# Second pass of a routed filter and expert kernel: earlier preparation of tiles, another order on the gather queue, results stored from the gathered row's buffer

## The chip, the core and the metric

The kernel runs on one core of a Trainium2 chip. The metric is the device time of one execution in microseconds (us). The kernel before was timed three times, and its median is compared with that of the changed kernel.

## What is computed

Input `x` has 16 x 1024 tokens of 512 numbers. Every token is normalised, then goes two ways: through a filter in the frequency domain with a Golay code correction on top of it (`s`), and through the two best of eight experts (`g`). Cut to what matters:

```python
xn = _layernorm(x)
# attention part: a circular filter whose response depends on D, a number from the data
x1 = ifft(fft(xn) * filt(D)).real
bits = (sigmoid(x1 @ W_el + b_el) > 0.5)              # 24 bits a token
s = x1 + golay_correct(bits) @ W_le + b_le
# expert part
probs = softmax(xn @ router_w.T)                      # 8 experts
topk_vals, topk_idx = top_k(probs, 2)
w = topk_vals / (topk_vals.sum() + 1e-6)
ffn = sum over the two chosen e of (xn @ expert_weights[e] + probs[e]) * w[e]
out = x + s * silu(ffn)
```

## The kernel before, in words

**First pass (`pass_1`, lines 919 to 1016).** It streams `x` in 32 blocks, filters every token, works out bits and routing, and leaves three things in DRAM: the filtered rows `yd`, a record of 28 numbers for each token (`recd`: the eight expert weights, the mean, the scale, the bias, the corrected bits) and, for each of the 28 pairs of experts, a list of the tokens that chose it (`lists`). The lists are then read as one order of tokens, pair after pair. `bounds_b` (line 848) and `place_q` (line 855) compute from the counts where place q of that order stands in `lists`: `place_q` does so for 16 tiles of 128 tokens at a time, on DVE.

**Second pass (lines 1023 to 1247).** It works on 128 tiles of 128 tokens in that order. Neighbouring pairs share an expert, so that a tile needs few experts: there are 283 (tile, expert) items, two for each tile and 27 more. The main loop (line 1212) has one turn `i` for each item; `t = i // 2` is the tile that is about to be prepared, and `f = t - 14` the tile that is finished, because the items lag by up to 14 tiles. All engines' instructions are in the order in which this loop emits them (`manual_schedule`), and each engine takes its own in order. What one tile needs, by engine:

- **POOL** issues five indirect DMAs a tile in even turns: the tile's token numbers (`fetch_tok`, `AHEAD_R` = 8 tiles ahead), its rows of `x` and its records (`fetch_x`, `AHEAD_X` = 5 ahead), the filtered rows of the tile that is soon finished (`fetch_y`), and the store of the last finished tile (`put`).
- **DVE** copies the index column for `fetch_tok` (`at`, line 1058), normalises (`normalize`, `AHEAD_N` = 3 ahead), opens the accumulator row (`open_tile`: weights copied, a memset), adds each product into it (line 1141), triples the bits (`triple`), adds the code's part to the filtered row (`mend`, line 1171), and builds the result in six instructions (`combine`, lines 1176 to 1181). Every 16 tiles it runs `place_q`.
- **PE** transposes the normalised tile (`turn`, four transposes, `AHEAD_T` = 2 ahead), does the item's product (line 1133: eight matmul records), transposes the bits into `pc` (`turn_code`, line 1160) and multiplies the corrected bits with `wle3` (`mend`, line 1170).
- **ACT** copies transposed tiles into a ring (`enter`), copies an item's tile out of the ring (`take`, `TAKES` = 3 items ahead), copies `pc` to `ct` (line 1164) and applies silu (`gate`).

The dynamic choices (which expert, which ring place) are register values that PE, ACT and DVE load from SBUF for four items at a time (`load_regs`, line 1108).

**Buffers that matter.** Products and the code product `pw` share five PSUM buffers (`ps_e`), `pc` has one (`ps_c`), transposed tiles two (`ps_x`). In SBUF: 20 buffers for gathered rows (`xg`), 2 for normalised rows (`xn2`), 3 for results (`o`), 27 for records and token numbers, 4 for item copies (`xw`, one more than `TAKES`), 2 for tripled bits.

**Order inside a turn before.** Even turns: (`place_q` every 16 tiles), `fetch_tok`, `fetch_x`, `fetch_y`, `put`, `normalize`, `turn`; then `take`, `enter`, `product`, `turn_code(f)`. Odd turns: `open_tile`, `take`, `product`, `triple(f + 1)`, `mend(f)`, `gate(f)`, `combine(f)`. So the bits of tile f are tripled in the odd turn before, transposed at the end of the even turn, and `mend(f)` needs them, through ACT's `ct`, one product later.

Of the kernel before, what the change touches and what calls it, by code (L numbers as in the profile page):

```python
# [8 lines left out]
F32 = mybir.dt.float32  # L9
BF16 = mybir.dt.bfloat16  # L10
U32 = mybir.dt.uint32
I32 = mybir.dt.int32
# [5 lines left out]
P = 128  # L18
PSUM = bass.MemoryType.PSUM
DRAM = bass.MemoryType.DRAM  # L20
NPAIR = 28
RING = 16
META = 28
# [27 lines left out]
def kernel(  # L51
# [29 lines left out]
    nc = tc.nc  # L81

    E = x.shape[-1]
    H = E // 2
# [8 lines left out]
    NT = N // P  # L93
# [3 lines left out]
    Q = E // 4  # L97
# [5 lines left out]
    bt = ctx.enter_context(tc.tile_pool(name="bt", bufs=1))  # L103
# [19 lines left out]
    mid = p1.enter_context(tc.tile_pool(name="mid", bufs=1))  # L123
# [17 lines left out]
    dbase_r = row_sb[:, NPAIR : 2 * NPAIR]  # L141
# [688 lines left out]


    G = 16
    addrs = [bt.tile([P, G], I32, name=f"addr{t}") for t in range(NT // G)]
    qf = bt.tile([P, NT], F32, name="qf")
    off = bt.tile([P, 3 * NPAIR], F32, name="off")
    step = bt.tile([P, NPAIR], F32, name="step")
    woff = bt.tile([1, NIP], I32, name="woff")
    slot = bt.tile([1, NIP], I32, name="slot")
# [1 line left out]
    md = Group()  # L840
# [7 lines left out]
    def bounds_b():  # L848

        po = ps_g.tile([P, 512], F32, name="pg")[:, 0 : 3 * NPAIR]  # L850
        nc.tensor.matmul(po, md.cnt, ord_sb, start=True, stop=True)
        nc.vector.tensor_copy(off, po)
        nc.vector.tensor_sub(step, dbase_r, off[:, 2 * NPAIR :])

    def place_q(t: int):

        cmp = bt.tile([P, G, NPAIR], F32, name="cmp")
        nc.vector.tensor_tensor(
            cmp,
            qf[:, t : t + G].unsqueeze(2).to_broadcast([P, G, NPAIR]),  # L860
            off[:, 0:NPAIR].unsqueeze(1).to_broadcast([P, G, NPAIR]),
            ALU.is_ge,
        )
        nc.vector.tensor_mul(cmp, cmp, step.unsqueeze(1).to_broadcast([P, G, NPAIR]))
        jump = bt.tile([P, G], F32, name="jump")
        nc.vector.tensor_reduce(jump, cmp, AX.X, ALU.add)
        nc.vector.tensor_add(addrs[t // G], jump, qf[:, t : t + G])

    def takes_a():

        begin, end = off[:, 0:NPAIR], off[:, NPAIR : 2 * NPAIR]
        lo = mid.tile([P, NPAIR], F32, name="lo")
        nc.vector.tensor_scalar(lo, begin, tf[:, 0:1], None, ALU.max)
        hi = mid.tile([P, NPAIR], F32, name="hi")
        nc.vector.tensor_scalar(hi, end, tf[:, 1:2], None, ALU.min)
        nc.vector.tensor_tensor(lo, lo, hi, ALU.is_lt)
        use = mid.tile([P, NE, NPAIR], F32, name="use")
        nc.vector.tensor_mul(use, mem_r, lo.unsqueeze(1).to_broadcast([P, NE, NPAIR]))
        md.takes = mid.tile([P, NE], F32, name="takes")
        nc.vector.tensor_reduce(md.takes, use, AX.X, ALU.max)  # L880
        takes_b = mid.tile([P, NE], BF16, name="takes_b")
        nc.vector.tensor_copy(takes_b, md.takes)

        md.pn = ps_g.tile([P, 512], F32, name="pg")[:, 0:NE]
        nc.tensor.matmul(md.pn, tri_b, takes_b, start=True, stop=True)
# [33 lines left out]
    def pass_1():  # L919
# [84 lines left out]
        bounds_a()  # L1004
        syndrome()
        bounds_b()
        place_q(0)
        correct()
        push(99)
        put_records(NT - GT, GT)  # L1010
# [10 lines left out]


    mp = ctx.enter_context(tc.tile_pool(name="mp", bufs=27))
    xnp = ctx.enter_context(tc.tile_pool(name="xnp", bufs=2))
    xgp = ctx.enter_context(tc.tile_pool(name="xgp", bufs=20))
    w2 = ctx.enter_context(tc.tile_pool(name="w2", bufs=2))
    rings = ctx.enter_context(tc.tile_pool(name="rings", bufs=1))
    ps_x = ctx.enter_context(tc.tile_pool(name="ps_x", bufs=2, space=PSUM))
# [2 lines left out]
    xring = rings.tile([P, RING, KC * P], F32, name="xring")  # L1031
    aring = rings.tile([P, RING, E], F32, name="aring")
    wring = rings.tile([P, RING * 16], F32, name="wring")
    nc.vector.memset(wring, 0.0)

    class Tile:
# [4 lines left out]
    def gather(dst, src, idx, limit):  # L1041
        nc.gpsimd.indirect_dma_start(  # L1042
            out=dst,
            out_offset=None,
            in_=src,
            in_offset=bass.IndirectOffsetOnAxis(ap=idx, axis=0),
            bounds_check=limit - 1,
            oob_is_err=False,
        )
# [12 lines left out]
    def fetch_x(t: int):  # L1062
        k = tiles[t]
        k.x = xgp.tile([P, E], F32, name="xg")
        gather(k.x, xf, k.tok, N)
        k.rec = mp.tile([P, META], F32, name="rec")
        gather(k.rec, recd, k.tok, N)

    def fetch_y(t: int):
# [4 lines left out]
    def normalize(t: int):  # L1074
        k = tiles[t]
        k.xn = xnp.tile([P, E], F32, name="xn2")
        nc.vector.tensor_scalar(  # L1077
            k.xn, k.x, k.rec[:, 10:11], k.rec[:, 11:12], ALU.subtract, ALU.mult
        )
# [9 lines left out]
    def enter(t: int):  # L1089

        nc.scalar.copy(xring[:, t % RING, :], tiles[t].pt)

    def open_tile(t: int):
        k = tiles[t]
        s = t % RING
        nc.vector.tensor_copy(wring[:, s * 16 : s * 16 + NE], k.rec[:, 0:NE])
        nc.vector.memset(aring[:, s, :], 0.0)
# [52 lines left out]
    def triple(t: int):  # L1150

        k = tiles[t]
        k.b3 = w2.tile([P, 3, 32], BF16, name="b3")
        bits = k.rec.bitcast(BF16)[:, BITS : BITS + 32]
        nc.vector.tensor_copy(k.b3, bits.unsqueeze(1).to_broadcast([P, 3, 32]))

    def turn_code(t: int):
        k = tiles[t]
        pc = ps_c.tile([96, P], F32, name="pc")
        nc.tensor.matmul(  # L1160
            pc, k.b3.rearrange("p k l -> p (k l)"), ident_b, start=True, stop=True
        )
        k.ct = w2.tile([96, P], BF16, name="ct")
        nc.scalar.copy(k.ct, pc)  # L1164
# [7 lines left out]

    def combine(t: int):
        k = tiles[t]
        k.o = w2.tile([P, E], F32, name="o", bufs=3)
        nc.vector.tensor_add(k.o[:, 0:Q], k.y[:, 0:Q], k.y[:, Q:H])
        nc.vector.tensor_sub(k.o[:, Q:H], k.y[:, 0:Q], k.y[:, Q:H])
        nc.vector.tensor_sub(k.o[:, H:E], k.o[:, 0:H], k.y[:, H:E])
        nc.vector.tensor_add(k.o[:, 0:H], k.o[:, 0:H], k.y[:, H:E])  # L1179
        nc.vector.tensor_mul(k.o, k.o, aring[:, t % RING, :])  # L1180
        nc.vector.tensor_add(k.o, k.o, k.x)  # L1181

    def put(t: int):
        k = tiles.pop(t)
        dma = nc.gpsimd.indirect_dma_start(  # L1185
            out=of,
            out_offset=bass.IndirectOffsetOnAxis(ap=k.tok, axis=0),
            in_=k.o,
            in_offset=None,
            bounds_check=N - 1,  # L1190
            oob_is_err=False,
        )
        tc.declare_no_dep(dma.ins, group="rows", reason="rows of their own")
        tc.add_to_no_dep_group("rows", dma.ins)

    LAST = NPAIR // 2
    AHEAD_R, AHEAD_X, AHEAD_N, AHEAD_T, TAKES = 8, 5, 3, 2, 3
    with tc.manual_schedule():
        for t in range(AHEAD_R):
            fetch_tok(t)  # L1200
            if 2 <= t and t - 2 < AHEAD_X:
                fetch_x(t - 2)
        load_regs(0)
        for t in range(AHEAD_N):
            normalize(t)
            if t < AHEAD_T:
                turn(t)
                enter(t)
        open_tile(0)
        for i in range(TAKES):  # L1210
            take(i)
        for i in range(NI + 2 * LAST):
            t = i // 2
            f = t - LAST
            if i % (2 * G) == 0 and t + G < NT:
                place_q(t + G)
            if i % 4 == 0 and i + 4 < NIP:
                load_regs(i + 4)
            if i % 2 == 0:
                if t + AHEAD_R < NT:  # L1220
                    fetch_tok(t + AHEAD_R)
                if t + AHEAD_X < NT:
                    fetch_x(t + AHEAD_X)
                if 0 <= f + 2 < NT:
                    fetch_y(f + 2)
                if 0 <= f - 1 < NT:
                    put(f - 1)
                if t + AHEAD_N < NT:
                    normalize(t + AHEAD_N)
                if t + AHEAD_T < NT:  # L1230
                    turn(t + AHEAD_T)
            elif t + 1 < NT:
                open_tile(t + 1)
            if i + TAKES < NI:
                take(i + TAKES)
            if i % 2 == 0 and t + AHEAD_T < NT:
                enter(t + AHEAD_T)
            if i < NI:
                product(i)
            if i % 2 == 0 and 0 <= f < NT:  # L1240
                turn_code(f)
            if i % 2 == 1 and 0 <= f + 1 < NT:
                triple(f + 1)
            if i % 2 == 1 and 0 <= f < NT:
                mend(f)
                gate(f)
                combine(f)
# [86 lines left out]
```

## Time and profile before

| what | value |
|---|---|
| three timed runs, us | 1593.53, 1586.84, 1565.13; median 1586.84 |
| the profiled execution's own time, us | 1558.99 |
| span of its trace, us | 1557.2 |
| mean granted TensorE clock | 0.964 |
| DVE / ACT / POOL busy, share of the span | 75% / 41% / 58% |
| product matmuls L1133 | 2264 records, 1021.3 us busy |
| one indirect DMA on POOL | about 1.0 us |
| DMA engines' mean busy share in the second pass | about 0.33 |

The page of the profile gives, for one execution, each engine's busy time, the span in 40 slices, and groups of instructions with their mean duration in ns. Other answers of the trace list the instructions in order of time: start, duration, engine, line, operation, "out<-in", how many, and in brackets how long the engine had been idle and what ended that ("issue": nothing that the profile shows; "remote": a signal whose sender the profile could not name). The ends of PE's matmuls are modelled, their starts are measured. The first pass fills about 400 us of the span; the first product of the second pass starts at 410.1 us.

### The profile page before, as it was taken

How to read it: one execution, taken by the hardware profiler on the slowest of the kernel's cores; microseconds unless marked ns; L12 is line 12 of the kernel's file. 1: busy time of each engine (PE TensorE's matmuls, PEld its weight loads, DVE VectorE, ACT ScalarE, POOL GpSimd, SP SyncE). 2: the span in 40 equal slices, each digit the busy share in tenths (PEclk: the TensorE clock that was granted, in tenths of full speed). 3: DMA queues.
4: the chain of work that ended last, by engine and by line, in shares of the span. 5: the costliest groups of instructions: out<-in, count | busy, mean ns of one | idle time of the engine just before them, and what ended most of it. 6: DMA issues, size and time to landing. Idle time of an engine off the chain costs nothing.

```text
span 1557.2 us, 20298 instructions
## 1 busy us (share of the span) xinstructions
PE 1408.6 (90%) x4955; PEld 751.6 (48%) x4955; DVE 1168.0 (75%) x3057; ACT 636.2 (41%) x1346; POOL 898.1 (58%) x907
## 2 busy tenths in 40 slices
PE   3998988885699989989898997999999989999997
PEld 2877777663344444434344443444444444444443
DVE  7799999997433668778676866877688778887666
ACT  4988888662122323323232322332333233333221
POOL 1357776675644556656655665666576656664332
PEclk8999999997699999999999999999999999999999
DMA  5997667531111223323323332333233333332211
GB/s 219 330 317 242 216 209 218 169 115 58 46 44 43 77 90 104 106 94 91 103 83 95 105 104 70 101 105 104 83 105 98 101 90 104 106 115 83 81 68 61
DMA packets 91391, 185.04 MB, mean 119 GB/s; under 512 B 21998, under 2 KB 57710, under 8 KB 87182
## 3 DMA queue, kind: packets, MB, share of 16 engines
q0 software_dynamic: 43472, 104.51, 22.3%
q1 hardware_dynamic: 46702, 78.07, 15.2%
q10 hardware_dynamic: 1104, 1.17, 0.2%
q8 instruction: 44, 0.72, 0.2%
q14 instruction: 69, 0.57, 0.1%
HBM read 112.86 MB, written 70.84 MB: 118 GB/s over the span
## 4 chain that ended last, share of the span: by engine, by line
PE 58%; DVE 21%; issue 12%; ACT 3%; POOL 3%; another core or an unknown queue 2%; DVEq 1%; DMA 0%; ACTq 0%; POOLq 0%
PE pe L1133 47%; PE pt L1085 3%; PE py L548 2%; DVE sd L518 2%; DVE pp L466 2%; PE pe L1170 1%; POOL yg L1042 1%; POOL out L1185 1%; DVE sd L521 1%; DVE ex L573 1%; ACT no L483 1%; PE pt L530 1%; DVE o L1180 1%; PE py L545 1%
## 5 line engine op out<-in xcount | busy, mean ns | idle before, releaser
L1133 PE MATMUL pe<-w_sb,xw 128*128 x2264 | 1021.3, 601 | 0.0
L1133 PEld LDWEIGHTS pe<-w_sb,xw 128*128 128x128 f32 x2264 | 415.8, 193 | 463.6 <-issue 463.1
L1141 DVE SCALAR_TENSOR_TENSOR aring<-pe,wring,aring 128x512 f32 x283 | 211.8, 749 | 262.8 <-PE pe L1133 133.6
L1042 POOL DMA_INDIRECT tok<-lists,at x120 | 130.8, 1090 | 245.0 <-DVE at L1058 232.2
L1148 ACT ACTIVATE aring<-aring,rec 128x512 f32<-128x512 f32 x128 | 92.5, 723 | 439.0 <-DVE aring L1141 359.8
L1122 ACT COPY xw<-xring 128x512 f32 x283 | 172.5, 611 | 78.5 <-PE pe L1133 58.6
L1042 POOL DMA_INDIRECT yg<-yd,tok x128 | 135.7, 1060 | 107.8 <-DVE o L1179 67.8
L795 POOL DMA_INDIRECT lists<-tok,dst x128 | 130.3, 1018 | 61.4 <-DVE mo L808 37.7
L1185 POOL DMA_INDIRECT out<-o,tok x128 | 132.5, 1035 | 54.0 <-issue 37.5
L1042 POOL DMA_INDIRECT xg<-in_x,tok x128 | 129.0, 1008 | 46.4 <-issue 39.6
L523 POOL TENSOR_TENSOR mm<-xt 128x256 f32<-128x256 f32 x128 | 99.8, 780 | 94.7 <-PE pt L530 58.3
L1042 POOL DMA_INDIRECT rec<-recd,tok x128 | 129.2, 1009 | 40.0 <-issue 39.7
L548 PE MATMUL py<-cm,pmt 128*128 128x288 f32 x512 | 149.1, 415 | 0.0
L1164 ACT CAST ct<-pc 96x128 bf16<-96x128 f32 x128 | 33.4, 261 | 268.7 <-PE pc L1160 157.9
L551 ACT ACTIVATE yb<-py,rec 128x640 f32<-128x640 f32 x128 | 101.5, 793 | 29.6 <-PE py L548 15.7
L548 PEld LDWEIGHTS py<-cm,pmt 128*128 128x128 f32 x512 | 92.5, 194 | 14.0
L1180 DVE TENSOR_TENSOR o<-o,aring 128x512 f32<-128x512 f32 x128 | 88.6, 692 | 14.0 <-issue 0.5
L1085 PEld LDWEIGHTS pt<-ident,xn 128*128 128x128 f32 x512 | 66.5, 147 | 66.8 <-issue 44.2
L1085 PE MATMUL pt<-ident,xn 128*128 128x128 f32 x512 | 82.4, 286 | 12.8 <-DVE xn L1077 9.3
L1181 DVE TENSOR_TENSOR o<-o,xg 128x512 f32<-128x512 f32 x128 | 88.8, 694 | 4.4
L483 ACT ACTIVATE no<-xt,sum 128x512 bf16<-128x512 f32 x128 | 91.0, 711 | 0.3 <-DVE pp L466 0.2
L1171 DVE TENSOR_TENSOR yg<-pe,yg 128x512 f32<-128x512 f32 x128 | 87.2, 681 | 0.0
(226 smaller groups left out, 1597.4 us busy)
## 6 DMA issues: line engine op xcount, KB each, us to landing
xt<-in_x SPq DMA_DIRECT2D x32, 1024.0 KB
yd<-yb SPq DMA_DIRECT2D x32, 1024.0 KB
w_sb<-in_expert_w SPq DMA_DIRECT2D x8, 1024.0 KB
lists<-tok,dst POOLq DMA_INDIRECT x128
xg<-in_x,tok POOLq DMA_INDIRECT x128
rec<-recd,tok POOLq DMA_INDIRECT x128
yg<-yd,tok POOLq DMA_INDIRECT x128
out<-o,tok POOLq DMA_INDIRECT x128
```

What stands on the lines that cost most here:

```text
L483: nc.scalar.activation(no, xts[g // TPT][:, g % TPT, :], AF.Square, bias=k.sum[:, j : j + 1], scale=-float(E), accum_out=k.sq2[:, j : j + 1],)
L523: nc.gpsimd.tensor_tensor(m, xr[:, 0:H], xr[:, H:E], ALU.subtract)
L548: nc.tensor.matmul(py[:, 1, 0 : X + H], pmt[:, 2 + c, :], cm[:, c, :], start=(c == 0), stop=(c == 1))
L551: nc.scalar.activation(y_room(g), py[:, :, 0:WY], AF.Copy, scale=k.rec[:, j, 11:12])
L795: dma = nc.gpsimd.indirect_dma_start(out=lists, out_offset=bass.IndirectOffsetOnAxis(ap=st.dst[:, j : j + 1], axis=0), in_=tok[:, t0 + j : ...
L1042: nc.gpsimd.indirect_dma_start(out=dst, out_offset=None, in_=src, in_offset=bass.IndirectOffsetOnAxis(ap=idx, axis=0), bounds_check=limit - 1,
L1085: nc.tensor.transpose(k.pt[:, c * P : (c + 1) * P], k.xn[:, c * P : (c + 1) * P], ident)
L1122: nc.scalar.copy(xw.rearrange("p c t -> p (c t)").unsqueeze(1), xring[:, bass.ds(regs.pop(("a", i)), 1), :],)
L1133: nc.tensor.matmul(pe.unsqueeze(1), xw[:, c, :], w_sb[:, bass.ds(e, 1), c, :], start=(c == 0), stop=(c == KC - 1),)
L1141: nc.vector.scalar_tensor_tensor(acc, pe.unsqueeze(1), wring[:, bass.ds(regs.pop(("c", i)), 1)], acc, ALU.mult, ALU.add,)
L1180: nc.vector.tensor_mul(k.o, k.o, aring[:, t % RING, :])
L1185: dma = nc.gpsimd.indirect_dma_start(out=of, out_offset=bass.IndirectOffsetOnAxis(ap=k.tok, axis=0), in_=k.o, in_offset=None, bounds_check ...
```

## The change

It moves preparation earlier and reorders the loop. Rows are normalised 4 tiles ahead instead of 3 and gathered 6 ahead instead of 5; items are copied 4 ahead instead of 3; bits are tripled three tiles before they are finished instead of one, and transposed one tile earlier (`CODE = 1`). The store `put(f - 1)` is emitted first in the even turn instead of after `fetch_y`, and `enter` comes before `take`. The result is built in one scratch row `mix`, and its last addition writes into `k.x`, the gathered row's own buffer, from which `put` stores; the three buffers `o` are gone. `place_q` uses `mix` (or a first-pass buffer) as its scratch and makes its addresses in two rotating buffers; `bounds_b` copies its sums in two instructions instead of one. Buffers: `xn2` 3, `xg` 22, `rec` 22, `xw` 5, `b3` 3.

```diff
-    addrs = [bt.tile([P, G], I32, name=f"addr{t}") for t in range(NT // G)]
+    addrs = {}
-    off = bt.tile([P, 3 * NPAIR], F32, name="off")
+    begin = bt.tile([P, NPAIR], F32, name="begin")
@@ bounds_b
-        nc.vector.tensor_copy(off, po)
-        nc.vector.tensor_sub(step, dbase_r, off[:, 2 * NPAIR :])
-
-    def place_q(t: int):
-        cmp = bt.tile([P, G, NPAIR], F32, name="cmp")
+        nc.vector.tensor_copy(begin, po[:, 0:NPAIR])
+        md.off = mid.tile([P, 2 * NPAIR], F32, name="off")
+        nc.vector.tensor_copy(md.off, po[:, NPAIR:])
+        nc.vector.tensor_sub(step, dbase_r, md.off[:, NPAIR:])
+
+    def place_q(t: int, room):
+        cmp = room[:, 0 : G * NPAIR].rearrange("p (g k) -> p g k", k=NPAIR)
+        jump = room[:, G * NPAIR : G * (NPAIR + 1)]
...
-        jump = bt.tile([P, G], F32, name="jump")
         nc.vector.tensor_reduce(jump, cmp, AX.X, ALU.add)
+        addrs[t // G] = bt.tile([P, G], I32, name="addr", bufs=2)
@@ buffers of the second pass
-    xnp = ctx.enter_context(tc.tile_pool(name="xnp", bufs=2))
-    xgp = ctx.enter_context(tc.tile_pool(name="xgp", bufs=20))
+    xnp = ctx.enter_context(tc.tile_pool(name="xnp", bufs=3))
+    xgp = ctx.enter_context(tc.tile_pool(name="xgp", bufs=22))
+    mix = rings.tile([P, E], F32, name="mix")
-        k.rec = mp.tile([P, META], F32, name="rec")
+        k.rec = mp.tile([P, META], F32, name="rec", bufs=22)
-        k.b3 = w2.tile([P, 3, 32], BF16, name="b3")
+        k.b3 = w2.tile([P, 3, 32], BF16, name="b3", bufs=3)
@@ combine, put
-        k.o = w2.tile([P, E], F32, name="o", bufs=3)
-        nc.vector.tensor_add(k.o[:, 0:Q], k.y[:, 0:Q], k.y[:, Q:H])
...
-        nc.vector.tensor_mul(k.o, k.o, aring[:, t % RING, :])
-        nc.vector.tensor_add(k.o, k.o, k.x)
+        nc.vector.tensor_add(mix[:, 0:Q], k.y[:, 0:Q], k.y[:, Q:H])
...
+        nc.vector.tensor_mul(mix, mix, aring[:, t % RING, :])
+        nc.vector.tensor_add(k.x, mix, k.x)
-            in_=k.o,
+            in_=k.x,
@@ the loop
-    AHEAD_R, AHEAD_X, AHEAD_N, AHEAD_T, TAKES = 8, 5, 3, 2, 3
+    AHEAD_R, AHEAD_X, AHEAD_N, AHEAD_T, TAKES = 8, 6, 4, 2, 4
+    CODE = 1
             if i % (2 * G) == 0 and t + G < NT:
-                place_q(t + G)
+                place_q(t + G, mix)
             if i % 2 == 0:
+                if 0 <= f - 1 < NT:
+                    put(f - 1)
                 if t + AHEAD_R < NT:
                     fetch_tok(t + AHEAD_R)
                 if t + AHEAD_X < NT:
                     fetch_x(t + AHEAD_X)
                 if 0 <= f + 2 < NT:
                     fetch_y(f + 2)
-                if 0 <= f - 1 < NT:
-                    put(f - 1)
...
+            if i % 2 == 0 and t + AHEAD_T < NT:
+                enter(t + AHEAD_T)
             if i + TAKES < NI:
                 take(i + TAKES)
-            if i % 2 == 0 and t + AHEAD_T < NT:
-                enter(t + AHEAD_T)
             if i < NI:
                 product(i)
-            if i % 2 == 0 and 0 <= f < NT:
-                turn_code(f)
-            if i % 2 == 1 and 0 <= f + 1 < NT:
-                triple(f + 1)
+            if i % 2 == 0 and 0 <= f + CODE < NT:
+                turn_code(f + CODE)
+            if i % 2 == 1 and 0 <= f + CODE + 2 < NT:
+                triple(f + CODE + 2)
```

More of the change, by code (lines that the diff above doesn't have):

```diff
@@ L860, in place_q @@
             qf[:, t : t + G].unsqueeze(2).to_broadcast([P, G, NPAIR]),
-            off[:, 0:NPAIR].unsqueeze(1).to_broadcast([P, G, NPAIR]),
+            begin.unsqueeze(1).to_broadcast([P, G, NPAIR]),
             ALU.is_ge,
@@ L864, in place_q @@
         nc.vector.tensor_mul(cmp, cmp, step.unsqueeze(1).to_broadcast([P, G, NPAIR]))
-        jump = bt.tile([P, G], F32, name="jump")
         nc.vector.tensor_reduce(jump, cmp, AX.X, ALU.add)
+        addrs[t // G] = bt.tile([P, G], I32, name="addr", bufs=2)
         nc.vector.tensor_add(addrs[t // G], jump, qf[:, t : t + G])
     def takes_a():
-        begin, end = off[:, 0:NPAIR], off[:, NPAIR : 2 * NPAIR]
+        end = md.off[:, 0:NPAIR]
         lo = mid.tile([P, NPAIR], F32, name="lo")
@@ L1006, in pass_1 @@
         bounds_b()
-        place_q(0)
+        place_q(0, mid.tile([P, E], F32, name="cmp"))
         correct()
@@ L1174, in combine @@
         k = tiles[t]
-        k.o = w2.tile([P, E], F32, name="o", bufs=3)
-        nc.vector.tensor_add(k.o[:, 0:Q], k.y[:, 0:Q], k.y[:, Q:H])
-        nc.vector.tensor_sub(k.o[:, Q:H], k.y[:, 0:Q], k.y[:, Q:H])
-        nc.vector.tensor_sub(k.o[:, H:E], k.o[:, 0:H], k.y[:, H:E])
-        nc.vector.tensor_add(k.o[:, 0:H], k.o[:, 0:H], k.y[:, H:E])
-        nc.vector.tensor_mul(k.o, k.o, aring[:, t % RING, :])
-        nc.vector.tensor_add(k.o, k.o, k.x)
+        nc.vector.tensor_add(mix[:, 0:Q], k.y[:, 0:Q], k.y[:, Q:H])
+        nc.vector.tensor_sub(mix[:, Q:H], k.y[:, 0:Q], k.y[:, Q:H])
+        nc.vector.tensor_sub(mix[:, H:E], mix[:, 0:H], k.y[:, H:E])
+        nc.vector.tensor_add(mix[:, 0:H], mix[:, 0:H], k.y[:, H:E])
+        nc.vector.tensor_mul(mix, mix, aring[:, t % RING, :])
+        nc.vector.tensor_add(k.x, mix, k.x)
     def put(t: int):
```

## The prediction

> **What bounds the kernel now.** I read the page first, then the busy time by stage, PE's waits, the chain of waits and the instructions in order of time. Busy time by stage (PE, PEld, DVE, ACT, POOL, then clock, DMA share, GB/s):
>
> ```profile
> 410.00:541.00 131.00, 130.85 (x356) 60.96 (x355) 58.97 (x133) 34.98 (x59) 62.67 (x62) 0.98 0.19 51
> 541.00:1400.00 859.00, 811.81 (x2287) 377.60 (x2286) 646.63 (x1476) 269.69 (x521) 537.18 (x521) 0.98 0.33 98
> 1400.00:1547.00 147.00, 147.00 (x381) 65.55 (x379) 104.36 (x218) 41.01 (x81) 50.12 (x43) 1.00 0.23 76
> ```
>
> The second pass is bound by PE, which is without a gap before 541 us and after 1400 and loses 47 us between: just the stretch in which POOL issues all five DMAs a tile. An undisturbed tile takes 7.64 us of PE there, as two pieces of the chain of waits show (start, duration):
>
> ```profile
> 894.22 3.49 PE pe L1133 x8
> ...
> 901.86 3.49 PE pe L1133 x8
> ```
>
> The same view gives 7.31 us for the first 14 tiles, which finish none, and the order of time gives 7.20 at the end, without transposes. 14 x 7.31 + 112 x 7.64 + 15.5 x 7.20 = 1069.6 us; from the first product at 410.1 that ends at 1479.7. The last product really ends at 1547.1: **67 us lost**. After it 10.1 us of tail follow, so the floor of the span is 1490. PE's waits in this pass:
>
> ```profile
> PE pe L1170 <- issue: 27.3, 7, 4.8
> PE pe L1170 <- DVE aring L1141: 11.2, 2, 5.6
> PE pt L1085 <- DVE xn L1077: 4.2, 8, 3.0
> PE pc L1160 <- DVE b L1155: 2.3, 2, 1.7
> PE pe L1170 <- ACT ct L1164: 1.9, 1, 1.9
> ```
>
> Ten stops at the code product L1170 make 40.4 us, eight transposes and two bit transposes 6.5. The remaining 20 us are matmuls at half clock after stops. What ends a stop shows in the order of time:
>
> ```profile
> 666.00 1.13 POOL L1042 DMA_INDIRECT tok<-lists,at  x1 [4.13 <-DVE at L1058]
> ...
> 672.68 1.03 POOL L1042 DMA_INDIRECT tok<-lists,at  x1 [0.30 <-DVE xn L1077]
> ...
> 677.91 0.22 PE L1160 MATMUL pc<-ident_b,b 128*96 128x128 bf16 x1
> 677.97 3.65 PE L1133 MATMUL pe<-w_sb,xw 128*128 x8
> ...
> 684.58 1.01 POOL L1185 DMA_INDIRECT out<-o,tok  x1 [0.30 <-issue]
> 686.19 0.75 DVE L1141 SCALAR_TENSOR_TENSOR aring<-pe,wring,aring 128x512 f32 x1 [6.74 <-remote]
> 686.89 0.26 ACT L1164 CAST ct<-pc 96x128 bf16<-96x128 f32 x1 [10.08 <-remote]
> ...
> 687.21 0.61 PE L1170 MATMUL pe<-wle,ct 96*128 96x512 bf16 x1 [5.59 <-DVE aring L1141]
> ```
>
> PE finished the product and `pc` at 678.1, yet DVE and ACT, both idle, act on it only at 686.2 and 686.9. So PE's signal is held for 8 us, PE does the next product, and then waits for `ct`, not for DVE as the bracket says: two of five `ps_e` buffers are taken. Each of the ten stops has such a hold beside it. What they share is POOL: a tile's five DMAs start 1.31 us apart (6.54 us); in quiet tiles POOL then waits 0.77 or 1.8 us for DVE's `at`. Here `place_q` made it wait 4.13, it fell behind, and 15 DMAs ran without a pause (19.6 us) until 685.6. The signals came 0.6 us later. Six long runs follow `place_q`, the others an odd pause of POOL or an earlier hold. That a long run causes the hold is my inference; the trace has no row for it.
>
> **What the Trainium skill says.** (1) *Perfetto Trace Analysis*, "Tensor Engine Instruction (MATMUL, LD_WEIGHTS)": the end of a matmul is estimated, and its signal goes out only once PSUM has acknowledged the write. That permits a late signal; an 8 us one no page explains. (2) *TensorE: Matmul & The Clock Gate*, "What's actually happening": the clock halves after an idle window of about 3.4 us and recovers after a busy one. The trace agrees: after the stop above, the four transposes take 1.06 us against 0.60. (3) *GPSIMD Engine Reference*, "4. When to use GPSIMD": POOL's cores themselves write the descriptors of its DMAs; here 1.0 us of POOL for each. (4) *DMA: Bandwidth & Descriptors*, "Anatomy of one DMA — SWDGE (gpsimd) path": 2.0 us plus bytes / 436e3. My estimate for a 256 KB store is 2.6 us; no view here gives the landing.
>
> **The change part by part.**
>
> *Bits a tile earlier.* `mend(f)` no longer needs the `pc` of the same tile. After a hold begins at `pc`, PE does as before one product, then also `mend` (0.22), transposes (0.44) and the next product (3.44), before the next `pc` needs the single `ps_c` buffer, which ACT has not emptied. That is 4.1 us more cover. The ten stops are 4.83, 5.59, 1.86, 4.84, 4.83, 5.58, 2.71, 2.50, 2.74 and 4.84; less 4.1 each, at least nothing, 5.9 us stay. **Saved: 34.5.** The cover needs `xw` four ahead (ACT is held too) and `xn` made a tile before: both are in the change. PSUM allows five products or code products. If the cover were gone, the 34.5 would be back.
>
> *Normalised rows a tile earlier.* The 6.5 us of PE's waits on `xn` and bits come when `place_q` (0.62 x 3 + 0.17 = 2.0 us) delays DVE by about 3 us; the new lead is 7.6. **Saved: 6.5.**
>
> *Half clock.* With stops under 1.5 us PE should not cool: of the 20 us I take **17**; bounds 0 and 20.
>
> *Result in `mix`, store from `xg`.* The same six DVE instructions, no DMA removed. New wait: `fetch_x(t + 6)` needs the buffer whose store was issued in the tile before, seven DMAs (9.2 us) earlier; it lands after an estimated 2.6. Cost 0, hidden by those DMAs; if landing took over 9 us, POOL's rows, records and `yg` behind it would be late too. `mix` has only DVE as its user, in order: 0.
>
> *`put` first.* It waits for DVE's last addition L1181, and `fetch_tok` (then `xg`, `rec`, `yg`) is queued behind; but `at` follows L1181 on DVE anyway, so nothing is later. After `place_q` the store fills part of the pause: I work out store, pause of 1.9, four DMAs, pause of 1.4, then ten without a pause (12.9 us) and one of 0.8, instead of fifteen. SP has no part in this pass; ACT's queue only swaps `enter` and `take`, and `take` now waits for the transposes, which precede the product: 0. `yg` goes 1.3 us later in a tile and is needed two tiles on: 0.
>
> *One more small copy at the end of the first pass.* The nearest row, COPY of 128x8, has 197 ns: +0.2. Two more DMAs in the prologue (2.6 us) lie beside the first five products (17 us).
>
> *What is late next.* After a hold PE no longer paused, so DVE is up to 7.5 us behind (the product's 3.44 and the 4.1). A DVE-bound tile takes 6.5 us (L1181 starts at 671.46 and 677.92), so DVE regains 1.1 a tile; meanwhile POOL (6.54) runs without pause, and a new hold may follow. The trace shows such followers: the holds of 746, 1084 and 1215, where PE stopped least, each had another 26 to 28 us later. Bounds: 0, and the second rival. I charge **20 us**, about a third of the way.
>
> Sum: 1557.2 - 34.5 - 6.5 - 17 + 20 + 0.2 = 1519 span; with the 1.8 us around it 1521 against 1558.99. The timed median lies 28 us above that execution. I take this surplus for more holds and carry over a small part, 4 us, because each costs less: **1525**.
>
> **Rivals.**
> - *Nothing follows.* Without the 20 us: 1505. For it: most holds follow `place_q`, whose run is broken up. I count it with the forecast: together 0.55, between 1495 and 1545.
> - *Holds follow each other.* POOL runs 12 us until the hold, DVE lives 7.5 on older signals, the begun tile ends: four tiles (26.1) and a pause of 6.5 until DVE's next L1181. 8.15 us a tile: 112 x 0.51 = 57 over the floor, 1490 + 57 + 2 = 1549. For it: the followers above. Against it: `rec` or `xg` pauses break runs. 0.22, 1545 to 1575.
> - *No effect.* Leads are useless because DVE, held as well, fills `ps_e`: about 1587. Against it: three free buffers at the stop. 0.08.
> - *Slower.* POOL becomes the bound: DVE stands from the beginning of each hold, three tiles (19.6) and a pause of 6.5, 8.70 us a tile: 112 x 1.06 = 119, 1611, plus cold clock up to 1650. It decides above 8.49 us a tile, where 1586.84 is reached. Against it: a DVE that is behind has old signals to work on. 0.15.
>
> **Numbers.** The likeliest is 1525, its own range 1495 to 1545; all cases give 1495 to 1600, with about 1.5 in 10 outside. A measurement of this kernel tells about 2% from no change: under 1555 is faster, 0.55 + 0.4 x 0.22 = 0.64; over 1618 slower, 0.6 x 0.15 = 0.09; the same 0.27.
>
> **What would show it.** Right: stops at L1170 below 10 us in all, PE over 97% between 541 and 1400, no wait on `xn` or bits, few half-clock slices, holds still there ("remote" before L1141), the run after `place_q` ten DMAs. Wrong: new long waits of PE at L1160, L1133 or L1170, POOL without pauses, tiles of 8.1 us or more, or POOL waiting before `xg` for a store.

## The result, and the profile after

The changed kernel took 1555.37 us (median of 20 runs, 1532.4 to 1568.6), the kernel before beside it 1585.01: 1.9% less, where I forecast 1525 and 3.9%. Over the undisturbed executions alone the ratio is 0.986 (95% interval 0.982 to 0.990), a gain of 1.4%; the profiled execution (1557.48 us, span 1555.7) counts as disturbed by that rule, but it lies 2 us from the median and is read as typical. The engines are called by their names in the profile: PE is TensorE, DVE VectorE, ACT ScalarE, POOL GpSimd.

Busy time by stage of the changed kernel (columns as in the prediction):

```profile
410.00:541.00 131.00, 131.00 (x359) 61.18 (x358) 61.39 (x139) 36.12 (x63) 66.16 (x65) 0.99 0.21 54
541.00:1400.00 859.00, 818.93 (x2287) 379.44 (x2286) 646.10 (x1471) 262.18 (x517) 537.25 (x519) 0.97 0.33 97
1400.00:1547.00 147.00, 145.81 (x376) 64.86 (x375) 106.59 (x222) 42.04 (x84) 44.26 (x44) 1.00 0.24 76
```

The middle stretch holds the same 2287 records of PE as before: the two profiled executions (1558.99 and 1557.48 us) are nearly equal, and the 30 us between the medians are not in these traces. I expected PE above 97% there; it has 95.3%. The waits in that stretch before (us in total, times, longest):

```profile
POOL tok L1042 <- DVE at L1058: 177.8, 81, 9.1
...
ACT ct L1164 <- remote: 87.3, 11, 10.1
...
DVE aring L1141 <- remote: 65.5, 14, 6.7
```

And after:

```profile
DVE aring L1145 <- remote: 109.9, 23, 8.3
ACT ct L1168 <- remote: 102.0, 16, 10.9
POOL out L1188 <- DVE xg L1184: 89.3, 16, 8.3
...
POOL out L1188 <- DVE at L1062: 72.2, 19, 8.4
...
PE pc L1164 <- ACT ct L1168: 31.7, 8, 6.1
```

The stops at the code product are gone, and stand one instruction earlier, at the bit transpose L1164, whose single PSUM place ACT has not emptied. The waits for held signals ("remote") have grown: 110 us before DVE's L1145 and 102 before `ct`, against 65.5 and 87.3. And POOL, which used to wait a little in most tiles, now waits rarely and long. In order of time:

```profile
575.35 1.12 POOL L1188 DMA_INDIRECT out<-xg,tok  x1 [5.28 <-DVE at L1062]
...
582.04 1.18 POOL L1188 DMA_INDIRECT out<-xg,tok  x1 [0.30 <-issue]
...
588.79 1.02 POOL L1188 DMA_INDIRECT out<-xg,tok  x1 [0.30 <-issue]
...
595.37 1.07 POOL L1188 DMA_INDIRECT out<-xg,tok  x1 [0.30 <-issue]
...
603.82 0.75 DVE L1145 SCALAR_TENSOR_TENSOR aring<-pe,wring,aring 128x512 f32 x1 [8.27 <-remote]
603.85 0.26 ACT L1168 CAST ct<-pc 96x128 bf16<-96x128 f32 x1 [4.42 <-remote]
604.17 0.26 PE L1164 MATMUL pc<-ident_b,b 128*96 128x128 bf16 x1 [3.27 <-ACT ct L1168]
...
610.12 1.13 POOL L1188 DMA_INDIRECT out<-xg,tok  x1 [8.41 <-DVE at L1062]
```

Four tiles of POOL without a pause (20 DMAs until 601.7), a hold, a stop of PE, DVE late, POOL waits 8.41 us for it, and the next run begins. Between 541 and 1340 us, 25 runs of eleven to twenty DMAs (gaps under 0.45 us) hold 423 of POOL's DMAs; before, 13 runs of ten to fifteen held 172. This is the prediction's rival "holds follow each other".

### The profile page after: what moved, and what is told of

It reads as the page before. It is cut to its first block, busy times and chain, and to the rows that moved or that the text cites. A ratio compares the mean times of both kernels' runs of the same rounds, so it can differ in the third digit from the quotient of the medians.

```text
span 1555.7 us, 20156 instructions
## 1 busy us (share of the span) xinstructions
PE 1415.1 (91%) x4955; PEld 754.2 (48%) x4955; DVE 1169.9 (75%) x3058; ACT 630.9 (41%) x1346; POOL 896.4 (58%) x907
## 4 chain that ended last, share of the span: by engine, by line
PE 48%; DVE 22%; issue 15%; another core or an unknown queue 5%; POOL 4%; ACT 4%; DVEq 1%; DMA 0%; POOLq 0%; ACTq 0%
PE pe L1137 38%; PE py L548 2%; PE pt L1089 2%; POOL yg L1046 2%; DVE sd L518 2%; DVE pp L466 2%; DVE aring L1145 2%; DVE sd L521 1%; ACT no L483 1%; DVE ex L573 1%; DVE mix L1183 1%; PE pt L530 1%; PE pe L1174 1%; PE py L545 1%
## 5 line engine op out<-in xcount | busy, mean ns | idle before, releaser
L1137 PE MATMUL pe<-w_sb,xw 128*128 x2264 | 1034.3, 607 | 1.2 <-DVE aring L1145 1.2
L1145 DVE SCALAR_TENSOR_TENSOR aring<-pe,wring,aring 128x512 f32 x283 | 211.8, 749 | 258.4 <-remote 111.2
L1188 POOL DMA_INDIRECT out<-xg,tok x128 | 137.4, 1073 | 290.9 <-DVE xg L1184 182.1
L1046 POOL DMA_INDIRECT tok<-lists,at x120 | 124.8, 1040 | 85.6 <-DVE at L1062 53.1
L1095 ACT COPY xring<-pt 128x512 f32<-128x512 f32 x128 | 73.1, 571 | 102.8 <-PE pt L1089 44.2
L1183 DVE TENSOR_TENSOR mix<-mix,aring 128x512 f32<-128x512 f32 x128 | 88.6, 692 | 14.7 <-DVE mix L1182 0.9
L1184 DVE TENSOR_TENSOR xg<-mix,xg 128x512 f32<-128x512 f32 x128 | 88.8, 694 | 4.4
L1175 DVE TENSOR_TENSOR yg<-pe,yg 128x512 f32<-128x512 f32 x128 | 87.3, 682 | 4.0 <-remote 2.4
```

What stands on the lines that cost most here:

```text
L1046: nc.gpsimd.indirect_dma_start(out=dst, out_offset=None, in_=src, in_offset=bass.IndirectOffsetOnAxis(ap=idx, axis=0), bounds_check=limit - 1,
L1137: nc.tensor.matmul(pe.unsqueeze(1), xw[:, c, :], w_sb[:, bass.ds(e, 1), c, :], start=(c == 0), stop=(c == KC - 1),)
L1145: nc.vector.scalar_tensor_tensor(acc, pe.unsqueeze(1), wring[:, bass.ds(regs.pop(("c", i)), 1)], acc, ALU.mult, ALU.add,)
L1183: nc.vector.tensor_mul(mix, mix, aring[:, t % RING, :])
L1188: dma = nc.gpsimd.indirect_dma_start(out=of, out_offset=bass.IndirectOffsetOnAxis(ap=k.tok, axis=0), in_=k.x, in_offset=None, bounds_check ...
```

## The experiments

**Theory H:** where POOL issues DMAs for longer than some 12 us without a pause, signals of PE are held; the change left PE no stop in which DVE catches up, so runs follow on runs. **Rivals:** C, the single PSUM place of the bit transpose is what costs; P, POOL's own work is the bound; L, the longer leads remove waits that have nothing to do with holds.

The experiments ran on different chips, and this proved to be the largest effect of all. I name the chips by the time of the *unchanged* kernel before, taken beside each experiment:

| chip | kernel before, us | experiments |
|---|---|---|
| A | 1579.6 | e1 to e4 |
| B | 1495.9, 1495.8 | e5 to e8, e13 to e15 |
| C | 1495.1, 1494.9 | e9 to e12, e17 |
| D | 1585.3 | e16 |
| E | 1565.6 | e18 |

B and C were met twice and gave the same time both times; A, D and E were met once each. Ratios below are to the kernel before on the same chip, with 95% intervals. The changed kernel itself was timed in two places only: for the result above, and on chip C. Where times on A, D and E are set against its 1555, that is across comparisons.

### On chip A: pause, fewer DMAs, second place, store first

**e1**, the changed kernel with a pause of POOL:

```diff
                 if t + AHEAD_R < NT:
+                    for _ in range(4):
+                        nc.gpsimd.memset(rest, 0)     # 128x16 scratch
                     fetch_tok(t + AHEAD_R)
```

> The changed kernel with four memsets of a 128x16 scratch by GpSimd ahead of each tile's fetch of its row numbers, so that GpSimd's DMAs never run on for more than one tile (five DMAs, 6.5 us) without 0.8 us or so between two of them. Theory H (GpSimd's uninterrupted run of DMAs, when longer than some 12 us, holds back the signals of TensorE; the change removed TensorE's stop and so let runs follow on runs): the waits of ScalarE and VectorE for a remote signal, 102 and 110 us, fall below 30 us, the stops of TensorE at the bit transpose (41 us) below 12, and the time falls from 1555 to 1490 to 1515. Rival C (the stops come from the single PSUM place of the bit transpose, whatever GpSimd does): the waits stay and the time is 1550 to 1570. Rival P (GpSimd's own work is the bound): 0.4 us more a tile makes it slower, about 1555 + 112 x 0.4 = 1600.

Measured: 1508.8 us, ratio 0.954 (0.947 to 0.961). No wait for a remote signal is left between 541 and 1400 us, PE is busy for 856 of 859 us at full clock, and POOL's DMAs come in fives with 1.31 us between:

```profile
541.00:1400.00 859.00, 856.17 (x2448) 399.09 (x2447) 697.29 (x1573) 282.47 (x557) 617.69 (x988) 1.00 0.35 103
```

With work added to POOL the kernel is 47 us below the change alone (ratio 0.954 here, 0.986 for the change beside its own kernel before). So P falls, and C falls as the cause of the holds: the waits went although the single place stayed.

**e2** leaves out the gather of the records from the 17th tile on and uses those of the first 16 again (`if t < 16: gather(k.rec, ...) else: k.rec = recs[t % 16]`), so that POOL issues four DMAs a tile:

> The changed kernel with the gather of the records left out from the 17th tile on (records of the first 16 tiles are used again, so the output's weights and corrections are those of other rows). GpSimd issues four DMAs a tile, 5.2 us, in place of five, 6.5. Theory H: GpSimd has over 1.5 us a tile to wait, so no run is long, the holds go, and the time is 1485 to 1515. Rival C: as the changed kernel, 1545 to 1565. Rival P (GpSimd's work is the bound): also faster, near 1490, so this run tells H and P from C only; the pause run tells H from P.

Measured: 1494.4, ratio 0.946 (0.939 to 0.953); no remote wait, PE busy for 859.00 of 859 us. As H expects.

**e3**, `ps_e` 5 to 4 buffers, `ps_c` 1 to 2:

> The changed kernel with two PSUM places for the bit transpose and four, in place of five, for the products. Rival C: the stops at the bit transpose (41 us) go and the time falls to about 1515 to 1525. Theory H: a hold of about 8 us still stops TensorE at the next place it needs (four products' places now last 2.2 us less), so the sum of TensorE's waits stays at 40 to 60 us and the time within 1545 to 1570.

Measured: 1542.4, ratio 0.979 (0.970 to 0.987). The stops at L1164 are gone, but PE now stops at the products, 22.8 us for ACT's `xw` and 9.1 for DVE's accumulation. The waits for remote signals stay (99.8 us before DVE's L1145, 60.3 before `ct`). The place decides where PE stops, not whether a hold comes. H's numbers were a little high: PE's waits come to 32 us where I expected 40 to 60, and the time, 13 us under the 1555 of the changed kernel, is slightly below H's range and well above C's.

**e4**, the kernel before with only `put` moved to the front:

> The kernel before with one edit of the change alone: the store of a finished row is issued first among a tile's DMAs instead of last. My prediction put the gain of the change on the longer leads and counted the order of the store as small: 1575 to 1590 expected. A rival: the store's wait for VectorE now stands ahead of all fetches, breaks GpSimd's runs differently and takes a good part of the change's 30 us: 1555 to 1570. A third: without the longer leads it makes more pauses and fewer holds but delays fetches: 1590 to 1610.

Measured: 1529.1, ratio 0.970 (0.962 to 0.978): better than the whole change and below all three expectations. Held signals are much shorter here:

```profile
DVE aring L1141 <- remote: 41.6, 13, 5.0
...
ACT ct L1164 <- remote: 20.6, 6, 6.5
```

Six of its long runs are of ten DMAs (about 13.2 us), among them those after `place_q` at 665.84, 794.58 and 1174.41, as the prediction had worked out for the store's move. But eleven others have 14 to 20 DMAs, and its 17 runs of ten or more hold 236 DMAs between 541 and 1340 us, more than the 172 of the kernel before. A run of twenty (723.3 to 750.6) held one signal of DVE for 4.1 us and stopped PE not at all. So H in the form of run lengths does not explain why e4 is fast; that stays open.

### Chips without holds

**e5**, the change with `put` back behind `fetch_y` (leads and `mix` without the store's move); **e6**, before + pause; **e7**, before + store first + pause; **e8**, the change with `CODE = 0`:

> The changed kernel with the store put back to the end of a tile's DMAs, as in the kernel before: the longer leads and the scratch row without the move of the store. The store's move alone gave 1529, less than the whole change (1555). Theory H: the leads take TensorE's stop away, and that stop was what let VectorE catch up and GpSimd pause; with the store last as well there are the fewest pauses, so the holds follow each other: 1570 to 1600, no gain over the kernel before. Rival L (the leads are worth 26 us or more by themselves, as my prediction worked out, and the two edits only overlap): 1525 to 1560.

> The kernel before with the four memsets of GpSimd ahead of each tile's row numbers, and nothing else. Theory H: without long runs of GpSimd's DMAs there are no holds and nothing for the longer leads to cover; the time is that of the changed kernel with the pause, 1500 to 1520. Rival L (the short leads stop TensorE by themselves): ten stops at the code product and the waits for normalised rows stay, 1540 to 1570.

> The kernel before with the store first and with the pause: next to the changed kernel with the pause (1509) it differs by the longer leads and the scratch row only. Theory H: 1500 to 1520, the leads are worth under 10 us when nothing is held. Rival L: 1525 to 1545.

> The changed kernel with the bit transpose back in the tile of its code product, all other leads as changed. If the earlier bit transpose is the lead that lets runs follow on runs (TensorE again stops at the code product in a hold), the time comes near that of the store's move alone: 1520 to 1540. If another lead does it (rows gathered and normalised a tile earlier), it stays at 1545 to 1570.

All four met chip B, where the kernel before took 1495.9. Measured: e5 1493.6 (0.998), e6 1517.2 (1.014), e7 1511.8 (1.011), e8 1493.5 (0.998). So where nothing is held, the leads are worth 2 us, and the pause *costs* 16 to 21. The expectations for e5 and e8 were meant for a chip with holds and aren't tested by this; e6 and e7 came within H's numbers and below L's, but where nothing is held that says nothing about holds.

**e9**, the changed kernel as it is; **e10**, **e11** and **e12** repeat e5, e8 and e6:

> The changed kernel as it is, beside the kernel before on the chip of this call. The chips of the two calls so far differ: on the first the kernel before took 1580 and signals of TensorE were held, on the second it took 1496 and GpSimd's runs of up to 15 DMAs (20 us) held nothing. Theory H': the hold is this chip's answer to GpSimd's long runs, and the change's gain is only what it saves of the holds. Where the kernel before takes 1496, expected 1488 to 1497 (under half a per cent); where it takes 1580, 1550 to 1560. Rival L (the leads remove waits that have nothing to do with holds): 15 us or more also where the kernel before takes 1496.

> The changed kernel with the store back at the end of a tile's DMAs, again, for the chip where signals are held. Theory H there: the leads alone give 1560 to 1600, since TensorE's stop no longer lets VectorE catch up and GpSimd pause. Rival L there: 1525 to 1560. On a chip without holds: 1491 to 1496, as before, which tells nothing new.

> The changed kernel with the bit transpose in the tile of its code product, again, for the chip where signals are held. If the earlier bit transpose lets runs follow on runs: 1520 to 1540 there; if another lead does it: 1545 to 1570. On a chip without holds: 1491 to 1496.

> The kernel before with GpSimd's pause, again, for the chip where signals are held. Theory H there: 1508 to 1525, the same as on the chip without holds (1517), since a pause a tile leaves nothing to hold. If the holds have another origin: above 1540 there.

On chip C: e9 1493.7, ratio 0.9995 (0.9986 to 1.0004), e10 1493.5, e11 1492.8, e12 1516.0. So **on this chip the change is worth nothing that can be measured**, and L falls. In e9 PE never stops:

```profile
541.00:1400.00 859.00, 859.00 (x2463) 401.96 (x2462) 693.89 (x1580) 289.97 (x562) 557.97 (x541) 1.00 0.35 104
```

It has long runs of POOL too, seven with 13 to 20 DMAs, six of them soon after a `place_q`, and here they hold nothing. They are fewer than the 25 of the first trace of the same kernel (107 DMAs against 423): so most of the long runs there seem to be themselves a consequence of holds, which make DVE late and POOL wait and then run on. The run that begins at 666.43 has 15 DMAs, 19.9 us; near its end:

```profile
666.43 1.13 POOL L1188 DMA_INDIRECT out<-xg,tok  x1 [1.37 <-DVE at L1062]
...
679.07 0.26 ACT L1168 CAST ct<-pc 96x128 bf16<-96x128 f32 x1 [1.51 <-PE pc L1164]
...
685.16 1.18 POOL L1046 DMA_INDIRECT yg<-yd,tok  x1 [0.30 <-issue]
686.71 0.26 ACT L1168 CAST ct<-pc 96x128 bf16<-96x128 f32 x1 [1.51 <-PE pc L1164]
687.27 1.01 POOL L1188 DMA_INDIRECT out<-xg,tok  x1 [0.93 <-DVE xg L1184]
```

`ct` waits 1.51 us, and the view names PE's `pc` as the sender instead of "remote". The name alone proves little, since "remote" only says that the profile found no sender; the lengths do. Over the whole stretch:

```profile
ACT ct L1168 <- PE pc L1164: 157.3, 107, 1.7
DVE aring L1145 <- PE pe L1137: 111.6, 96, 2.1
```

**e13** asked whether a still longer run would hold signals here: the row numbers are fetched a second time into a scratch that nothing reads.

```diff
         gather(k.tok, lists, at, NPAIR * N)
+        if t >= AHEAD_R:
+            gather(mp.tile([P, 1], I32, name="tok3", bufs=2), lists, at, NPAIR * N)
```

> The changed kernel with a sixth DMA a tile on GpSimd: the row numbers are fetched a second time into a scratch that nothing reads. GpSimd then needs 6 x 1.31 = 7.86 us a tile, more than the 7.63 of TensorE, so its runs of DMAs have hardly a pause over a whole stage. Theory H' (holds are a property of the chip: on some, no run of any length holds a signal): on a chip where the kernel before takes 1496, no wait for a remote signal and 1494 + 112 x 0.23 = 1515 to 1530, the plain cost of GpSimd as the bound; on one where it takes 1580, above 1600. Rival T (a hold comes on every chip, only after longer runs than the 27 us seen without one): waits for a remote signal and above 1550 also where the kernel before takes 1496.

> The leads without the move of the store, a third time, for the chip where signals are held: there 1560 to 1600 by theory H (the leads take away the stop that let GpSimd pause), 1525 to 1560 by rival L (the leads cover the stops). Elsewhere 1491 to 1496.

> The bit transpose in the tile of its code product, all other leads as changed, a third time, for the chip where signals are held: there 1520 to 1540 if the earlier bit transpose is the lead that lets runs follow on runs, 1545 to 1570 if it is another. Elsewhere 1491 to 1496.

Again chip B: e13 1537.0 (1.029; 1.026 to 1.032), e14 1492.9, e15 1492.7. In e13 POOL issued 632 DMAs between 541 and 1400 us with no gap over 0.31 us, not one wait for a remote signal appears, and PE's clock stays at 1.00:

```profile
541.00:1400.00 859.00, 835.28 (x2360) 384.20 (x2359) 668.88 (x1512) 267.86 (x534) 666.32 (x633) 1.00 0.34 100
```

POOL is the plain bound: 859 / 632 = 1.36 us a DMA, 8.2 us a tile. The expected 1515 to 1530 was low because I had taken 1.31. T falls: length alone does not bring a hold.

### Back on chips with holds

**e16**, the edit of e5:

> The leads without the move of the store, once more, for a chip where signals are held (the kernel before near 1580): there 1560 to 1600 by theory H (the leads take away TensorE's stop, which let VectorE catch up and GpSimd pause, and the store last adds no pause), 1525 to 1560 by rival L (the leads cover the stops and gain by themselves what my prediction gave them). Where the kernel before takes 1496: 1491 to 1496.

Chip D: 1494.4, ratio 0.947 (0.940 to 0.955). H as I had stated it expected 1560 to 1600, and L 1525 to 1560: both missed. The trace shows a pause that I had not counted. POOL's order in one tile, and what it waits for between 541 and 1400 us:

```profile
605.67 1.02 POOL L1188 DMA_INDIRECT out<-xg,tok  x1 [0.30 <-issue]
606.99 1.03 POOL L1046 DMA_INDIRECT tok<-lists,at  x1 [0.30 <-issue]
609.28 1.16 POOL L1046 DMA_INDIRECT xg<-in_x,tok  x1 [1.26 <-DMA out<-xg,tok]
```

```profile
POOL xg L1046 <- DMA out<-xg,tok: 80.2, 84, 2.5
```

With results stored from the gathered row's buffer, 22 buffers and the store last, the gather of a row needs the buffer of the store issued two DMAs ahead of it and waits for its landing. Its pauses break POOL's DMAs into fives; no run has more than six. With the store first, as in the change, that store is seven DMAs old when the gather comes, nothing waits, and the runs grow. I had overlooked a pause that the experiment itself put in. PE is busy without a gap in that stretch, as it is with the same kernel on chips B and C (1492.9 to 1493.6).

**e17** and **e18** test this form of H: keep the change, store first, and take away one buffer.

```diff
-    xgp = ctx.enter_context(tc.tile_pool(name="xgp", bufs=22))
+    xgp = ctx.enter_context(tc.tile_pool(name="xgp", bufs=21))
```

> The changed kernel with 21 buffers for gathered rows in place of 22, nothing else. The leads alone ran at 1494 on a chip where the kernel before took 1585, against what theory H expected: there the gather of a row waits some 0.95 us in every tile for the landing of the store from the same buffer, issued two DMAs earlier, and that wait breaks GpSimd's run. The store moved first lands before the gather of the next tile needs its buffer, and the pause is gone. With one buffer fewer the gather needs the buffer of the store of its own tile. Theory H with this pause: on a chip where the kernel before is near 1580, waits of the gather for the store in most tiles, few or no waits for a remote signal, and 1490 to 1510, 45 to 65 under the changed kernel with 22. Rival O (the order of the store itself, not the pause, lets the holds come): 1545 to 1570 there. Where the kernel before takes 1496: 1491 to 1500.

> The changed kernel with 21 buffers for gathered rows in place of 22, again, for a chip where TensorE's signals are held. The gather waited for the store in 103 tiles, 108 us in all, on the chip of the last call, so the pause a tile is there. Theory H with this pause: where the kernel before is near 1580, few or no waits for a remote signal and 1490 to 1510. Rival O (the order of the store lets the holds come): 1545 to 1570 there. Where the kernel before takes 1496: 1491 to 1500.

e17 met chip C: 1493.4 against 1494.9 (0.9988; 0.998 to 0.9995). e18 met chip E: **1494.6 against 1565.6, ratio 0.958 (0.951 to 0.965)**. Waits and busy time of e18 between 541 and 1400 us:

```profile
POOL xg L1046 <- DMA out<-xg,tok: 72.7, 74, 2.4
...
DVE aring L1145 <- remote: 11.7, 6, 3.8
...
ACT ct L1168 <- remote: 8.5, 4, 3.4
```

```profile
541.00:1400.00 859.00, 859.00 (x2463) 401.37 (x2462) 695.82 (x1581) 291.23 (x561) 577.83 (x541) 1.00 0.35 104
```

One buffer fewer turns the change into a kernel that takes 1493 to 1495 on both chips it met, one without holds and one with. The order of the store as such (rival O, 1545 to 1570) is not the cause; what counts is whether POOL pauses in each tile. On E this version beats the kernel before, and, across chips of like times before, the change too.

## Why the prediction was wrong

**The floor was right.** I put it at a span of 1490; on chip C the changed kernel has 1491.8, with PE at 7.64 us a tile.

**The failed step is "What is late next".** It took it that a new hold follows in a part of the cases only, because DVE mostly catches up first, and charged 20 us, "about a third of the way" to the second rival. With the other terms as they stood the sum is 1557.2 - 34.5 - 6.5 - 17 + 0.2 = 1499.4, so the measured span of 1555.7 leaves 56 for that term. Holds did follow each other nearly everywhere. Scaling the floor's 7.64 us a tile by PE's records in the stretch (2463 in e9, 2287 in the change) gives 8.23 us; the rival said 8.15 and 1549. I had the mechanism and the price, and gave it a chance of 0.22. My own numbers, DVE at 6.5 us a tile when behind and POOL at 6.54, said that POOL finds no pause while DVE catches up; that should have made this the likeliest case.

**Bits a tile earlier, half clock.** This is the same loss seen from PE, and is not to be added to the 56. The stops left L1170 and came back at L1164: 38.0 us (31.7 for `ct`, and the two smaller groups of 3.3 and 3.0) in place of 40.4. The cover was there, but the signals came later too: from the start of a bit transpose to that of `ct` it is 9.0 us at most before and 13.6 after. PE now has 7.5 us of work in that time (the 3.44 of a product and the 4.1), so 6.1 are left, and 6.1 is the longest stop in the view. So neither the 34.5 nor the 17 came in; the clock in the stretch is 0.97 where it was 0.98, and 1.00 in e9. Booked this way, with 2.4 and 0 for the two terms, about 7 us would be left for what is late next.

**Normalised rows.** No wait of PE for `xn` is left between 541 and 1400 us: right, 4 to 6 us.

**Result in `mix`, `put` first.** Both were costed at 0, and each was judged by the time that its own wait takes. The buffer wait that I named was hidden, as I said (the store's landing, estimated at 2.6 us, has a median of 2.9 in e9, well under 9.2). Where it does come, it works as a *pause* and is worth about 60 us: 1494.6 (e18) against the change's 1555.4, in different comparisons. The store's move was not worth 0: alone it gave 51 us on chip A (e4), for a reason that run lengths don't explain. "Ten DMAs after `place_q`" was right in e4 after four of six `place_q`; in the changed kernel DVE is behind by then, and the run at 679.26 has twenty.

**My inference** that a long run of POOL causes the hold was right as far as this: on chips A, D and E, four different ways to break the runs (a memset, a DMA fewer, the store's buffer with the store last, and with it first) each had at most 22 us of waits for remote signals between 541 and 1400 us, against 233 in the first trace of the changed kernel, and took 1494 to 1509. It was incomplete: the long run is needed, and so is the chip, and e4 shows long runs that held little. I still take the 28 us by which the timed median before exceeded its profiled run for more holds, but only one of these executions has a trace. On chips without holds that kernel takes 1495; by that measure holds cost 64 us in the profiled run and about 90 in the median.

**What stays open.** What in a chip makes the hold, and what holds the signal, no run shows. One rival is untested: the recording itself. The traces of the chips with holds contain fewer semaphore events, for the same kernel: the changed kernel's first trace has 11227 and its trace on chip C 19386 (4629 and 5671 in the first 400 us already); the kernel of e16 has 13214 on D and 19295 on B. A sender can thus be "remote" there because its record is missing, and whatever loses the records may also delay the signals. Every timed execution has a recorded span and clock, so no run shows whether holds come without recording. Why the store's move alone gave 51 us (e4) is open. That the longer leads took away PE's stops and so let runs follow on runs is my reading of the traces: which of the leads does it was not settled, since e8, e11 and e15 met chips without holds. The kernel before with a pause was not seen on a chip with holds either.

## What to carry to other kernels

When a stall recurs beside an engine that issues DMAs without a pause, do not only cover the stall: here 4.1 us more cover left the stops as long as they were. Try a short pause for the issuing engine, and look for one that is free, such as a buffer that comes back just in time. Time a kernel on more than one chip before you tune against a wait whose sender the profile cannot name.

## What the runs showed of the hardware

- Chips differed by 5 to 6% on the same kernel: the kernel before took 1566 to 1585 on three of them and 1495 to 1496 on two. With a pause of POOL in every tile the difference was gone: the kernel of e16 took 1494.4 on D and 1492.9 to 1493.6 on B and C, that of e18 1494.6 on E and 1493.4 on C.
- On chip B, 632 indirect DMAs of GpSimd, 859 us without a gap over 0.31 us, left no wait for a remote signal. On chips with holds, runs of 10 to 20 (13 to 27 us) had waits of up to 10.9 us beside them, though not all alike: a run of 20 in e4 had one of 4.1.
- A store of 128 rows of 2 KB let the next user of its buffer start 3.6 us after the store's own start (605.67 to 609.28 in e16; 3.3 in the median of the stretch).
- Four memsets of 128x16 take 4 x 0.12 us (e1), but widened the gap in GpSimd's DMAs from 0.30 to 1.31 us in most tiles; the four together take 0.63 us there, and the next fetch starts 0.67 us after them.
